# A graph layer on one core: rows of x by ScalarE's queue for five groups more, the sigmoid of the distances further back, and two gather buffers fewer

## The chip, the cores and the metric

The kernel runs on one core of a Trainium2 chip. The metric is the device time of one execution in microseconds (us), lower is better; the time of a kernel is the median of several executions. The core has five engines that run side by side: TensorE (PE; its weight loads are listed as PEld), VectorE (DVE), ScalarE (ACT), GpSimd (POOL) and SyncE (SP). An engine works through its own instructions in order. Transfers (DMAs) are issued by SP, ACT or POOL and announce their landing by semaphores.

## The reference

One message-passing layer over a graph with N = 12500 nodes and 200000 edges that are sorted by their target, followed by a residual and a layer norm. ssp(x) is softplus(x) - ln 2.

```python
gates = ssp(edge_attr @ We1 + be1) @ We2 + be2
gates = gates * (1 - sigmoid(5 * (distance - 3.5)))
h = ssp(concat(x[src], x[dst]) @ Wn1 + bn1) @ Wn2 + bn2
sums = zeros_like(x).at[dst].add(h * gates)
new = x + ssp(sums @ Ws1 + bs1) @ Ws2 + bs2
out = layernorm(x + new)
```

All is float32. `distance` is called `dist` in the kernel, and 1 - sigmoid of it is kept in the tile `cut`.

## The kernel before

**Groups.** Edges go in NG = 391 groups of 512, each as K = 4 columns of 128 edges. For group g the kernel needs the 512 rows x[src]: they go to a tile `xg` of 128 x 4 x 128 numbers, 64 of each 128 being a row of x, and 42 a one-hot code of the edge's target inside a window (`onehot`, L219). POOL fetches them by indirect DMA, one for each column (`gather`, L186), from the indices `src_i`. `gather` runs AHEAD = 16 groups in front of the group at work, and `xg` has AHEAD + BEHIND = 20 buffers. In one group of every 32 (the slots: 36, 68, ..., 388, twelve of them) only three columns are gathered. The 128 rows of the fourth are read by SP as plain DMAs of one row, ROWS = 4 in each step (`fetch`, L197 and L201), in the 32 steps before, to a tile `xr`; the row numbers come from the tile `rows_i` by a register load. In such a group `onehot` copies the code to `xr` (L221).

**A step** of the main loop works on several groups at once, in an order written out by hand. TensorE's order in step i is: second layer on the edges of group i-1 (L269, L272), first layer of group i+1 (L236, L238 on the edge data `eT`, L244 on the transposed rows with the weights `wns`), `scatter` of group i-3 (L295, messages times one-hot code), transposes of group i+3 (L227), second layer on the nodes of group i-1 (L278). ScalarE takes the exponential (L255) and logarithm (L258) of the first layer's result `z` and copies the transposed rows (L232). VectorE makes softplus of them (L263), multiplies by `cut` (L287) and by the gate (L291), adds the scatter's windows to `sums` (L311). SP loads `eT` (L207) and two pieces of `wns` (L214) for group i+5. `wns` holds, below the weights of the source, 42 rows of a table that the kernel itself writes to memory before the loop: the target's part of the first layer, for each node.

A buffer of `xg` is free once its group's scatter has ended. In step i POOL is to gather group i+16 to the buffer of group i-4, whose scatter stands in step i-1.

**Node blocks.** When all edges of a block of 512 nodes are done, the last part of the reference (`node_block`, L330 to L390) is strewn over the steps that follow.

**The start.** Before the loop DVE finds each group's window, ScalarE prepares biases, and TensorE computes the table in 14 pieces (PARTS = 7 parts of two, L508). ScalarE (L510) and DVE (L511) copy each piece from PSUM, SP stores it (L512), and DVE clears a stretch of `sums` (L513), where the input of that piece had lain. Gathers start here too: the first FREE = 7 groups at once, and the other nine of the AHEAD groups each behind a piece of the table, by a memset on DVE (L181) that the gather waits for:

```python
waiting.setdefault(min(5 * (g - FREE) // 3, 2 * PARTS - 1), []).append(g)
```

Ahead of the first piece stands the sigmoid of the distances (L498 to L501): DVE, ScalarE with a load of the sigmoid's table, a load of the table for exponential and logarithm, DVE. After the sixth piece (part 2) DVE computes the targets relative to their windows, `rel` (L524, L527).

Of the kernel before, what the change touches and what calls it, by code (L numbers as in the profile page):

```python
# [42 lines left out]
F32 = mybir.dt.float32  # L43
BF16 = mybir.dt.bfloat16
I32 = mybir.dt.int32
AF = mybir.ActivationFunctionType
OP = mybir.AluOpType
# [2 lines left out]
DRAM = bass.MemoryType.DRAM  # L50
DVE = mybir.EngineType.DVE
SP = mybir.EngineType.SP


Part = namedtuple("Part", "tensor others")

P = 128
D = 64
# [4 lines left out]
PIECES = 3  # L63
NB = 512
K = 4
AHEAD = 16
LOADS = 5
SPREADS = 5
CATCH_UP = 10
PREPARE = 5  # L70
FREE = 7
BEHIND = 4


BLOCK_STEPS = ((2, 3, 4, 4, 6, 7, 8, 9, 10, 14), (2, 3, 3, 4, 5, 6, 7, 8, 9, 10), (1, 2, 1, 2, 3))
ROWS = 4
CUTOFF = 5.0
EPS = 1e-5
LN2 = 0.6931471805599453
# [20 lines left out]

def slots_by_rows(NG):

    return [g for g in range(P // ROWS + 4, NG - 2, P // ROWS)]


@with_exitstack
def gnn_resnorm_kernel(ctx: ExitStack, tc: tile.TileContext, a: dict, out: bass.AP, E: int):
    nc = tc.nc
    x = a["x"]
    N = x.shape[0]  # L110
    NG = a["eT"].shape[1]
# [10 lines left out]
    loads = ctx.enter_context(tc.tile_pool(name="loads", bufs=LOADS + 2))  # L122
# [26 lines left out]
    packed, at = {}, 0  # L149
# [17 lines left out]

    xgs, xrs, eTs = {}, {}, {}

    by_rows = slots_by_rows(NG)  # L170
    rows_i = const.tile([len(by_rows), P], I32, name="rows_i")

    def padding(g, k):
# [13 lines left out]
                out=xg[:, k, :D], out_offset=None, in_=x,  # L187
                in_offset=bass.IndirectOffsetOnAxis(ap=src_i[:, g, k : k + 1], axis=0))

    def fetch(i):  # L190

        n, r = divmod(i * ROWS, P)
        if i < 0 or n >= len(by_rows):
            return
        if r == 0:
            xrs[by_rows[n]] = loads.tile([P, P], F32, name="xr", bufs=2)
        _, at = nc.values_load_multi_w_load_instructions(  # L197
            rows_i[n : n + 1, r : r + ROWS], engines=[SP], min_val=0, max_val=N - 1,
            skip_runtime_bounds_check_because="src holds rows of x")
        for j, v in enumerate(at):  # L200
            nc.sync.dma_start(xrs[by_rows[n]][r + j : r + j + 1, :D], x[bass.ds(v, 1), :])  # L201

    bases = {}

    def load(g):
# [195 lines left out]
    with tc.manual_schedule():  # L401
# [4 lines left out]
        with tc.tile_pool(name="prep", bufs=1) as prep:  # L406
# [14 lines left out]
            dist = cut.rearrange("p g k -> p (g k)")  # L421
# [52 lines left out]
            for i, w in enumerate((we2[:D, 0, :], wn2)):  # L474
                n = w.shape[0]
# [16 lines left out]
            rows = prep.tile([PIECES, 4, D], BF16, name="rows")  # L492
# [2 lines left out]
                load_x(i)  # L495


            nc.vector.tensor_scalar(dist, dist, CUTOFF - 1.5, 5.0, OP.subtract, OP.mult)  # L498
            nc.scalar.activation(dist, dist, AF.Sigmoid)
            nc.scalar.preload_act_table_set("natural_log_exp_and_others")  # L500
            nc.vector.tensor_scalar(dist, dist, -1.0, 1.0, OP.mult, OP.add)  # L501
            by_node = table.rearrange("(p c) f -> p c f", c=NCH)
            for i in range(PARTS):
                for c in range(i * CP, (i + 1) * CP, CP // 2):
                    m = CP // 2
                    ps = z_tile().rearrange("p b (k f) -> p (b k) f", k=K)
                    for k in range(m):
                        nc.tensor.matmul(ps[:, k, :], xT[:, c + k, :], wnb, start=True, stop=True)  # L508
                    tb = prep.tile([P, m, 2 * D], F32, name="tb", bufs=6)
                    nc.scalar.copy(tb[:, :K, :], ps[:, :K, :])  # L510
                    nc.vector.tensor_copy(tb[:, K:, :], ps[:, K:m, :])  # L511
                    nc.sync.dma_start(by_node[:, c : c + m], tb)  # L512
                    nc.vector.memset(sums[:, c * P : WIDE if c + m == NCH else (c + m) * P], 0.0)  # L513
                    for g in waiting.get(c // m, []):
                        gather(g, after=True)
                if i == 1:
                    nc.vector.tensor_copy(base_i, base_b[:1])
                    for k in range(2):
                        nc.vector.tensor_copy(be3[:, k, :], rows[:, 0, :])
                    for k in range(K):  # L520
                        nc.vector.tensor_copy(row3[:, :, k, :], rows[:, 1:3, :])
                        nc.vector.tensor_copy(rs3[:, k, :], rows[:, 3, :])
                if i == 2:
                    nc.vector.tensor_copy(rel, dst_i)  # L524
                    for t in range(2):
                        r = rel[:, :, 2 * t : 2 * t + 2]
                        nc.vector.tensor_sub(r, r, base_b[:, :NH].rearrange("p (g h) -> p g h", h=2))  # L527


        with tc.tile_pool(name="finish", bufs=1) as finish:  # L530
# [24 lines left out]
            for i in range(-3, last - 1):  # L555
                now = parts.pop(i, [])
                early = [part for part in now if part.tensor]
                at(load, i + LOADS)
                fetch(i)
                if i >= 0:  # L560
                    at(gather, i + AHEAD, i < BEHIND)
                if i < ends:
                    for g in second[i]:
                        layer2_edge(g)
                    if i >= -1:
                        zs[i + 1] = z_tile()
                        layer1_edge(i + 1)
                        for part in early:
                            part.tensor(tx_tile())
                    if i >= -1:  # L570
                        layer1_node(i + 1)
                    for n, g in enumerate(third[i]):
                        scatter(g, zs[i + 1][:, 1, HE + 2 * W * n : HE + 2 * W * (n + 1)])
                    at(exps, i + 1)
                    at(logs, i + 1)
                    for g in ahead[i]:
                        transposes(g)
                        xcopy(g)
                    for g in second[i]:
                        layer2_node(g)  # L580
                    for g in second[i]:
                        hcut(g)
                        message(g)
                    for g in third[i]:
                        window(g)
                    for part in early:
                        part.others()
                    at(softplus, i + 1)
                else:
                    for g in ahead[i]:  # L590
                        transposes(g)
                        xcopy(g)
                    zs[i + 1] = z_tile()
                    layer1_edge(i + 1)
                    for part in early:
                        part.tensor(zs[i + 1][:, 1, HE:])
                    layer1_node(i + 1)
                    exps(i + 1)
                    logs(i + 1)
                    for g in second[i]:  # L600
                        layer2(g)
                        hcut(g)
                        message(g)
                    softplus(i + 1)
                    for g in third[i]:
                        scatter(g, tx_tile()[:, : 2 * W])
                        window(g)
                    for part in early:
                        part.others()
                for g in ahead[i]:  # L610
                    at(onehot, g + 2)
                for part in now:
                    if not part.tensor:
                        part.others()
                complete = third[i][-1] + 1 if third[i] else 0
                if blocks and complete >= blocks[0][1] - PREPARE and not begun:
                    begun = node_block(*blocks[0][0], finish)
                    begun.pop(0).others()
                if blocks and complete >= blocks[0][1]:
                    steps = next(steps for steps in BLOCK_STEPS if i + steps[-1] < last - 1)  # L620
                    for n, part in zip(steps, begun):
                        parts.setdefault(i + n, []).append(part)
                    rest = begun[len(steps) :]
                    blocks.pop(0)
                    begun = None
# [38 lines left out]
            for part in begun:  # L664
# [4 lines left out]
                         skip_runtime_bounds_check_because="a comparison's result")  # L669
    with tc.If(far > 0), tc.tile_pool(name="outside", bufs=1) as o:  # L670
# [7 lines left out]
        with tc.For_i(0, NG, 1) as g:  # L678
# [14 lines left out]
            for k in range(K):  # L693
                for i in range(2):
                    nc.gpsimd.indirect_dma_start(
                        out=xg[:, k, i, :], out_offset=None, in_=x,
# [20 lines left out]
            v = gh.rearrange("p (i k d) -> p i k d", i=2, k=K)  # L717
# [27 lines left out]
def layouts(inputs):  # L745
# [3 lines left out]
    x = np.asarray(inputs["x"])  # L749
    src, dst = (np.asarray(inputs[n]) for n in ("src", "dst"))  # L750
    dist = np.asarray(inputs["edge_weight1"])[:, 0]
    edge = np.asarray(inputs["edge_attr_64"])
    N, E = x.shape[0], src.shape[0]
    NG = -(-E // GE)
# [9 lines left out]

    out = {"x": np.ascontiguousarray(x)}
    out["src_l"] = lanes(src, 0)
    out["rows"] = np.ascontiguousarray(out["src_l"].reshape(P, NG, K)[:, slots_by_rows(NG), K - 1].T)
    out["dst_l"] = lanes(dst, dst[-1])
    out["dist_l"] = lanes(dist, 1e6)
    out["dst_h"] = np.ascontiguousarray(padded(dst, NR * P * HE, dst[-1]).reshape(NR, P, HE).transpose(1, 0, 2))  # L770
# [4 lines left out]
    steps = block_steps(N, NG)  # L775
# [37 lines left out]
```

## Time and profile before

| what | value |
|---|---|
| time before, median of 3 runs | 2487.79 us (2479.47 to 2490.7) |
| the profiled execution | 2482.05 us, of which the span of the profile is 2480.3 us |
| mean granted TensorE clock | 0.861 |
| gathers on POOL (L186) | 1551, 950 ns each |
| rows by SP's plain DMAs (L201) | 1536 |
| first copy of a table piece, last copy | at 33.92 us, at 87.35 us |
| first and last exponential of the main loop's groups (L255) | at 99.34 us, at 2460 us |

A page gives each engine's busy time with its share of the span, the costliest groups of instructions (source line, engine, operation, tiles, count, then busy time, mean ns of one, idle time of the engine before them and what ended it), and the chain of work that ended last. A timeline's line starts with the start in us and the duration in us, and ends with the idle time before, in brackets, with what ended it; "remote" there is a release that the profile couldn't name. A table by stretches gives, for each stretch, its length, the busy time and number of instructions of PE, PEld, DVE, ACT and POOL, then the granted clock, the DMA share and GB/s. Starts of TensorE's matmuls are recorded, their ends modelled.

### The profile page before, as it was taken

The page shows a single profiled execution, that of the slowest core. Times are in us where ns is not written, and L with a number is a line of the kernel's source. Part 1 is how long each engine was busy: PE and PEld are TensorE (multiplying, and loading weights), DVE is VectorE, ACT ScalarE, POOL GpSimd, SP SyncE. Part 2 cuts the span into 40 slices and gives each one's busy share as a digit, 9 for nine tenths or more (in the row PEclk, how much of TensorE's full clock was granted, in tenths as well). Part 3 has the DMA queues.
Part 4 walks back from the last instruction along what each step waited for, and adds up shares of the span by engine and source line. Part 5 has one row for each costly group of instructions (what it writes and reads, how often), then busy time and mean ns, then how long its engine had stood idle before and what let it go on. Part 6 is the DMA issues. An engine that isn't in the chain of part 4 may idle for free.

```text
span 2480.3 us, 41084 instructions
## 1 busy us (share of the span) xinstructions
PE 2138.7 (86%) x11373; PEld 1741.1 (70%) x11373; DVE 1087.5 (44%) x2744; ACT 920.1 (37%) x1317; POOL 1473.3 (59%) x1555
## 2 busy tenths in 40 slices
PE   3888898889888989888988988888889888888897
PEld 3767677777767777767767776677767676676775
DVE  3334434444344344444444444444444444444455
ACT  1223333333333333433433333433333333433443
POOL 6656666666666666666666666666665656666620
PEclk9988879887888878898897888988887989988898
DMA  6322222222222222222222222222222222222220
GB/s 187 111 50 53 51 51 52 53 52 51 53 51 55 53 51 53 55 53 53 55 54 56 52 53 55 55 56 55 53 57 55 50 55 56 57 60 55 55 53 22
DMA packets 170982, 143.07 MB, mean 58 GB/s; under 512 B 46475, under 2 KB 142915, under 8 KB 170746
## 3 DMA queue, kind: packets, MB, share of 16 engines
q1 hardware_dynamic: 119746, 87.95, 12.3%
q0 software_dynamic: 49632, 50.92, 11.5%
q10 hardware_dynamic: 1368, 1.51, 0.3%
q8 instruction: 93, 1.52, 0.3%
q14 instruction: 143, 1.17, 0.2%
HBM read 130.57 MB, written 9.63 MB: 57 GB/s over the span
## 4 chain that ended last, share of the span: by engine, by line
PE 79%; issue 9%; DVE 5%; ACT 3%; another core or an unknown queue 3%; DVEq 1%; DMA 1%; SPq 0%; ACTq 0%
PE z L244 17%; PE gh L278 12%; PE gh L272 11%; PE z L238 11%; PE tx L227 8%; PE z L295 8%; PE gh L269 4%; PE z L236 3%; PE tx L330 2%; DVE h L287 1%; DVE msg L291 1%; ACT u L255 1%; DVE sums L311 1%; PE z L508 1%
## 5 line engine op out<-in xcount | busy, mean ns | idle before, releaser
L186 POOL DMA_INDIRECT xg<-in_x,src_i x1551 | 1473.1, 950 | 909.8 <-issue 360.3
L255 ACT ACTIVATE u<-z 128x768 f32<-128x768 f32 x392 | 317.4, 810 | 1435.4 <-PE z L244 466.8
L287 DVE TENSOR_TENSOR h<-gh,cut 128x256 f32<-128x256 f32 x391 | 166.0, 425 | 1154.0 <-PE z L244 357.8
L244 PE MATMUL z<-xT,wns 106*128 106x256 f32 x1564 | 498.4, 448 | 3.8 <-issue 1.6
L278 PE MATMUL gh<-consts,s 128*128 128x64 f32 x3128 | 429.6, 285 | 7.4 <-issue 7.4
L278 PEld LDWEIGHTS gh<-consts,s 128*128 128x128 f32 x3128 | 424.1, 210 | 6.9 <-issue 6.8
L272 PE MATMUL gh<-consts,s 128*128 128x128 f32 x1564 | 308.9, 325 | 133.8 <-issue 124.4
L244 PEld LDWEIGHTS z<-xT,wns 106*128 106x128 f32 x1564 | 353.0, 227 | 72.7 <-issue 4.2
L272 PEld LDWEIGHTS gh<-consts,s 128*128 128x128 f32 x1564 | 227.6, 210 | 240.4 <-issue 224.8
L263 DVE SCALAR_TENSOR_TENSOR s<-u,z 128x768 f32<-128x768 f32 x392 | 372.7, 951 | 24.3 <-ACT u L258 12.3
L258 ACT ACTIVATE u<-u,one 128x768 f32<-128x768 f32 x392 | 365.9, 934 | 12.7
L227 PE MATMUL tx<-consts,xg 128*106 128x128 f32 x1552 | 279.9, 308 | 61.0 <-ACT u L258 25.6
L238 PE MATMUL z<-eT,consts 128*128 128x256 f32 x782 | 313.9, 487 | 0.0
L295 PEld LDWEIGHTS z<-xg,msg 128*128 128x128 f32 x1512 | 279.8, 230 | 41.1 <-issue 8.2
L295 PE MATMUL z<-xg,msg 128*128 128x84 f32 x1512 | 263.4, 301 | 14.5 <-issue 14.2
L227 PEld LDWEIGHTS tx<-consts,xg 128*106 128x106 f32 x1552 | 211.3, 160 | 86.8 <-issue 46.0
L232 ACT COPY xT<-tx 106x512 f32<-106x512 f32 x391 | 221.6, 567 | 18.4 <-PE tx L227 11.2
L311 DVE TENSOR_TENSOR sums<-sums,z 64x42 f32 x756 | 148.7, 197 | 129.9 <-issue 118.4
L291 DVE TENSOR_TENSOR msg<-gh,h 128x256 f32<-128x256 f32 x391 | 165.8, 424 | 13.4
L238 PEld LDWEIGHTS z<-eT,consts 128*128 128x128 f32 x782 | 131.4, 211 | 54.1 <-issue 15.4
L269 PE MATMUL gh<-row,ones 3*128 3x512 bf16 x391 | 157.1, 402 | 2.7 <-DVE msg L291 2.6
L219 DVE TENSOR_TENSOR xg<-consts,rel 128x168 f32<-128x168 f32 x391 | 137.0, 351 | 0.1
(100 smaller groups left out, 621.4 us busy)
## 6 DMA issues: line engine op xcount, KB each, us to landing
eT<-in_eT SPq DMA_DIRECT2D x391, 128.0 KB
xg<-in_x,src_i POOLq DMA_INDIRECT x1551
xr<-in_x SPq DMA_DIRECT2D x1536, 0.2 KB
wns<-table SPq DMA_DIRECT2D x782, 21.0 KB
table<-tb SPq DMA_DIRECT2D x14, 448.0 KB
sums<-in_xT SPq DMA_DIRECT2D x7, 455.0 KB
y<-in_x SPq DMA_DIRECT2D x24, 128.0 KB
out<-y SPq DMA_DIRECT2D x24, 128.0 KB
```

What stands on the lines that cost most here:

```text
L186: nc.gpsimd.indirect_dma_start(out=xg[:, k, :D], out_offset=None, in_=x, in_offset=bass.IndirectOffsetOnAxis(ap=src_i[:, g, k : k + 1], ax ...
L227: nc.tensor.transpose(tx[:, k, :], row, ident)
L232: nc.scalar.copy(xT, xTs[g])
L238: nc.tensor.matmul(zs[g][:, 0, :HE], we1.rearrange("a h d -> a (h d)"), eTs[g], start=False, stop=True, skip_group_check=True)
L244: nc.tensor.matmul(zn, wns[:, g % REST, h, :], xTs[g][:, h], start=True, stop=True, skip_group_check=True)
L255: nc.scalar.activation(us[g][:, part], z_of(g)[:, part], AF.Exp)
L258: nc.scalar.activation(us[g][:, part], us[g][:, part], AF.Ln, bias=one)
L263: nc.vector.scalar_tensor_tensor(ss[g].rearrange("p i t e -> p (i t e)")[:, part], us[g][:, part], BIG, z_of(g)[:, part], OP.min, OP.max)
L269: nc.tensor.matmul(gh, ones3[:, :P], row3.rearrange("q i k d -> q (i k d)"), start=True, stop=False, skip_group_check=True)
L272: nc.tensor.matmul(v[:, 0, t], ss[g][:, 0, t, :], we2, start=False, stop=False, skip_group_check=True)
L278: nc.tensor.matmul(ghs[g][:, 1, 2 * t + h, :], ss[g][:, 1 + h, t, :], wn2, start=False, stop=h == 1 and t == 1, skip_group_check=True)
L295: nc.tensor.matmul(sc, msgs[g][:, 2 * t : 2 * t + 2, :].rearrange("p h f -> p (h f)"), xgs[g][:, 2 * t : 2 * t + 2, D:DW], start=t == 0, s ...
```

## The change

- Beside the slots that SP fills, ScalarE's queue fills others: one in every 64 groups, from group 69 (69, 133, 197, 261, 325), with ACT_ROWS = 2 rows of x in each step. `fetch` takes the queue as an argument; for ScalarE the row numbers of four steps (8) are loaded to registers at once. In these groups POOL gathers three columns too. Each of the two kinds has an `xr` tile of its own, with two buffers.
- AHEAD goes from 16 to 14, so `xg` has 18 buffers, and the first of the two loads of indices is for 14 groups. FREE goes from 7 to 5; nine groups still wait for table pieces.
- The sigmoid of the distances stands behind the table's sixth piece, ahead of `rel`.

```diff
-AHEAD = 16
+AHEAD = 14
-FREE = 7
+FREE = 5
+ACT_ROWS = 2
...
-    return [g for g in range(P // ROWS + 4, NG - 2, P // ROWS)]
+    return [list(range(P // n + 4 + (n == ACT_ROWS), NG - 2, P // n)) for n in (ROWS, ACT_ROWS)]
...
-    by_rows = slots_by_rows(NG)
+    sp_rows, act_rows = slots_by_rows(NG)
+    by_rows = sp_rows + act_rows
...
-    def fetch(i):
+    def fetch(i, slots, some, engine, queue, first, steps=1):
 
-        n, r = divmod(i * ROWS, P)
-        if i < 0 or n >= len(by_rows):
+        n, r = divmod(i * some, P)
+        if i < 0 or n >= len(slots):
             return
+        g = slots[n]
         if r == 0:
-            xrs[by_rows[n]] = loads.tile([P, P], F32, name="xr", bufs=2)
-        _, at = nc.values_load_multi_w_load_instructions(
-            rows_i[n : n + 1, r : r + ROWS], engines=[SP], min_val=0, max_val=N - 1,
-            skip_runtime_bounds_check_because="src holds rows of x")
-        for j, v in enumerate(at):
-            nc.sync.dma_start(xrs[by_rows[n]][r + j : r + j + 1, :D], x[bass.ds(v, 1), :])
+            xrs[g] = loads.tile([P, P], F32, name=f"xr{first}", bufs=2)
+        if i % steps == 0:
+            _, numbers[first] = nc.values_load_multi_w_load_instructions(
+                rows_i[first + n : first + n + 1, r : r + some * steps], engines=[engine], min_val=0, max_val=N - 1,
+                skip_runtime_bounds_check_because="src holds rows of x")
+        for j, v in enumerate(numbers[first][i % steps * some :][:some]):
+            queue.dma_start(xrs[g][r + j : r + j + 1, :D], x[bass.ds(v, 1), :])
...
-            nc.vector.tensor_scalar(dist, dist, CUTOFF - 1.5, 5.0, OP.subtract, OP.mult)
-            nc.scalar.activation(dist, dist, AF.Sigmoid)
-            nc.scalar.preload_act_table_set("natural_log_exp_and_others")
-            nc.vector.tensor_scalar(dist, dist, -1.0, 1.0, OP.mult, OP.add)
...
                 if i == 2:
+                    nc.vector.tensor_scalar(dist, dist, CUTOFF - 1.5, 5.0, OP.subtract, OP.mult)
+                    nc.scalar.activation(dist, dist, AF.Sigmoid)
+                    nc.scalar.preload_act_table_set("natural_log_exp_and_others")
+                    nc.vector.tensor_scalar(dist, dist, -1.0, 1.0, OP.mult, OP.add)
                     nc.vector.tensor_copy(rel, dst_i)
...
-                fetch(i)
+                fetch(i, sp_rows, ROWS, SP, nc.sync, 0)
+                fetch(i, act_rows, ACT_ROWS, ACT, nc.scalar, len(sp_rows), 4)
```

More of the change, by code (lines that the diff above doesn't have):

```diff
@@ L52 @@
 SP = mybir.EngineType.SP
+ACT = mybir.EngineType.Activation
 Part = namedtuple("Part", "tensor others")
@@ L168, in gnn_resnorm_kernel @@
     xgs, xrs, eTs = {}, {}, {}
-    by_rows = slots_by_rows(NG)
+    sp_rows, act_rows = slots_by_rows(NG)
+    by_rows = sp_rows + act_rows
+    assert len(set(by_rows)) == len(by_rows)
     rows_i = const.tile([len(by_rows), P], I32, name="rows_i")
@@ L188, in gather @@
                 in_offset=bass.IndirectOffsetOnAxis(ap=src_i[:, g, k : k + 1], axis=0))
-    def fetch(i):
-        n, r = divmod(i * ROWS, P)
-        if i < 0 or n >= len(by_rows):
+    def fetch(i, slots, some, engine, queue, first, steps=1):
+        n, r = divmod(i * some, P)
+        if i < 0 or n >= len(slots):
             return
+        g = slots[n]
         if r == 0:
-            xrs[by_rows[n]] = loads.tile([P, P], F32, name="xr", bufs=2)
-        _, at = nc.values_load_multi_w_load_instructions(
-            rows_i[n : n + 1, r : r + ROWS], engines=[SP], min_val=0, max_val=N - 1,
-            skip_runtime_bounds_check_because="src holds rows of x")
-        for j, v in enumerate(at):
-            nc.sync.dma_start(xrs[by_rows[n]][r + j : r + j + 1, :D], x[bass.ds(v, 1), :])
+            xrs[g] = loads.tile([P, P], F32, name=f"xr{first}", bufs=2)
[5 more added lines that the diff above has]
+            queue.dma_start(xrs[g][r + j : r + j + 1, :D], x[bass.ds(v, 1), :])
+    numbers = {}
     bases = {}
@@ L766, in layouts @@
     out["src_l"] = lanes(src, 0)
-    out["rows"] = np.ascontiguousarray(out["src_l"].reshape(P, NG, K)[:, slots_by_rows(NG), K - 1].T)
+    out["rows"] = np.ascontiguousarray(out["src_l"].reshape(P, NG, K)[:, sum(slots_by_rows(NG), []), K - 1].T)
     out["dst_l"] = lanes(dst, dst[-1])
```

## The prediction

> **What bounds the kernel now.** I read the page first, then the timeline of ScalarE (ACT) and GpSimd (POOL) over a few groups, then the busy times by stretch, then the start. The page suggests TensorE:
>
> ```profile
> PE 2138.7 (86%) x11373; PEld 1741.1 (70%) x11373; DVE 1087.5 (44%) x2744; ACT 920.1 (37%) x1317; POOL 1473.3 (59%) x1555
> PE 79%; issue 9%; DVE 5%; ACT 3%; another core or an unknown queue 3%; DVEq 1%; DMA 1%; SPq 0%; ACTq 0%
> L186 POOL DMA_INDIRECT xg<-in_x,src_i x1551 | 1473.1, 950 | 909.8 <-issue 360.3
> L255 ACT ACTIVATE u<-z 128x768 f32<-128x768 f32 x392 | 317.4, 810 | 1435.4 <-PE z L244 466.8
> ```
>
> The first exponential of each group (L255) marks the pace. POOL around step 180, where the group being gathered (196) is a slot that takes three gathers instead of four:
>
> ```profile
> 1191.49 0.94 POOL L186 DMA_INDIRECT xg<-in_x,src_i  x1 [1.40 <-PE z L236]
> 1192.74 0.95 POOL L186 DMA_INDIRECT xg<-in_x,src_i  x1 [0.30 <-issue]
> 1193.99 0.95 POOL L186 DMA_INDIRECT xg<-in_x,src_i  x1 [0.30 <-issue]
> 1195.24 0.94 POOL L186 DMA_INDIRECT xg<-in_x,src_i  x1 [0.31 <-issue]
> 1197.51 0.94 POOL L186 DMA_INDIRECT xg<-in_x,src_i  x1 [1.32 <-PE z L244]
> 1198.76 0.95 POOL L186 DMA_INDIRECT xg<-in_x,src_i  x1 [0.30 <-issue]
> 1200.01 0.94 POOL L186 DMA_INDIRECT xg<-in_x,src_i  x1 [0.30 <-issue]
> 1202.18 0.94 POOL L186 DMA_INDIRECT xg<-in_x,src_i  x1 [1.22 <-PE z L244]
> ```
>
> The busy times of the same three steps (cut at the starts of L255), and of three steps at the end when no gather is left:
>
> ```profile
> 1191.26:1197.27 6.01, 6.01 (x38) 5.04 (x37) 2.47 (x6) 2.53 (x4) 3.78 (x4) 1.00 0.23 51
> 1197.27:1201.94 4.67, 3.86 (x27) 3.18 (x26) 2.81 (x7) 2.22 (x3) 2.84 (x3) 1.00 0.19 35
> 1201.94:1208.03 6.09, 5.51 (x36) 4.55 (x36) 2.44 (x6) 2.62 (x6) 3.78 (x4) 1.00 0.22 51
> 2391.91:2396.26 4.35, 4.35 (x30) 3.66 (x29) 2.69 (x7) 2.22 (x3) 0.00 (x0) 1.00 0.20 58
> 2396.26:2401.06 4.80, 4.80 (x34) 4.11 (x33) 2.52 (x7) 2.54 (x5) 0.00 (x0) 1.00 0.16 44
> ```
>
> So a step's length follows the number of gathers: four 6.05 us (the median over the loop), three 4.67, none 4.35 to 4.80, with the clock at 1.00 in all of them. The slot steps 20, 52, 84, 116, 148, 180, 212, 244, 276 and 340 lie between 4.58 and 4.78. POOL issues every 1.25 us, then waits about 1.3 us for the scatter that frees its buffer; TensorE, ScalarE and POOL go on at the same moment. The work around it is elastic: steps with a node block's extra exponentials, or with its y load or its store on SP, have medians of 6.07, 6.05 and 6.02 us; only the step with L330 is longer (6.55).
>
> Where rule and trace part: the Trainium skill (Perfetto Trace Analysis, Identifying the Most-Contended Engine) calls the engine of highest occupancy the most contended, and counts weight loads for TensorE: 70% against POOL's 59%. By it a gather less is worth nothing. By the rows it is worth 6.05 - 4.68 = 1.37 us. I follow the rows; the rule's sum is a rival below.
>
> The start is the second place:
>
> ```profile
> 33.92 0.59 ACT L510 COPY tb<-z 128x512 f32<-128x512 f32 x1
> 41.30 0.59 ACT L510 COPY tb<-z 128x512 f32<-128x512 f32 x1 [6.80 <-remote]
> 53.99 1.07 ACT L510 COPY tb<-z 128x512 f32<-128x512 f32 x2 [12.10 <-remote]
> 87.35 0.59 ACT L510 COPY tb<-z 128x512 f32<-128x512 f32 x1 [2.40 <-PE z L508]
> ```
>
> These copies of table pieces wait for TensorE alone. Pieces 2 and 3 had ended by 24.2 and 38.5, yet their copies begin at 41.30 and 53.99. POOL gathers without a pause from 3.29 to 49.99 (7 free groups, then two that pieces 1 and 2 release), 36 gathers. Once it has paused, copies follow at 3.0 us, TensorE's pace. So a long run of gathers holds back the ends of matmuls as ScalarE sees them.
>
> **The change part by part.** (1) *Five slots more* (groups 69, 133, 197, 261, 325; the words say six, the list gives five): gathers fall from 1551 to 1546. 5 x 1.37 = **-6.9 us**. The five extra 0.19 us copies of L221 are beside other work.
>
> (2) *AHEAD 16 to 14*, with BEHIND at 4, so 18 buffers. POOL still waits for the scatter of four groups back, so the steady step stays. But the last gather is issued in step 376 instead of 374: two steps of 6.05 take the place of 4.80 and 4.35: **+3.0 us**.
>
> (3) *FREE 7 to 5*: eight gathers fewer before the table ends. The first run is 20 gathers, 3.3 to 28.3. POOL then idles until piece 1 is copied.
>
> (4) *Sigmoid behind the sixth piece*. ScalarE's stream has its rows DMA at 29.52, a table load that the build puts in (1.28 us, as before), then the first copy at 31.1 instead of 33.92. DVE writes the memset that frees the next gathers at about 33.1. Piece 2, its signal freed by POOL's pause, is copied at 32; piece 3 ends at 35.7, piece 4 at 38.8, each copied at once if eight gathers (33.4 to 43.4) are too few to hold signals back: before, some 13 gathers after the pause at 50 passed without harm (copies at 61.59 to 73.54 every 3.0 us), and the next copy came 3.2 us late (79.74). Then 3.0 us a piece: the sixth at 44.8. Now sigmoid: on ScalarE 1.28 + 1.51 + 1.28 us, with DVE's 0.98 on each side and its rel operations (0.97 + 1.86) behind; DVE copies piece 7 at 53.1 instead of 50, which makes TensorE 3.3 us late. Eight pieces follow, 24 us, with these 3.3 and some 4 us (0 to 9) of held signals: the last copy at about 76.3 (72 to 81) instead of 87.35: **-11 us**. The first reader of the result, L287, comes after 100 us.
>
> (5) *ScalarE's rows*: 640 one-row DMAs in 320 steps, two between the copy of xT and the next exponential, and a register load of eight numbers in every fourth. Row: SP's four take 2.6 to 3.4 us while POOL gathers, 1.5 without gathers, and the load before them 0.55. So ScalarE has 1.3 to 1.7 us a step and 0.6 more in every fourth. It idles 1435.4 / 392 = 3.66 us before the exponential: covered. If its two rows took over 3.6 us, each us beyond would cost 320. In a slot step the gap is 2.4 us: some 17 x 1/4 x 0.5 = 2 us at most. I take **+0.5**. Queued behind the rows are exponential, logarithm and copy; DVE's softplus, then TensorE's L272 and L244 wait for these.
>
> The rows share the eight landing semaphores with SP's loads: an ACT row mostly waits for an SP row of one step back, and 422 of SP's DMAs wait for an ACT row, most of one step back. SP loads five groups ahead (load k+5 leaves within 1.6 us of exponential k), so there are 30 us of cover. At the start there is less: SP's load k+5 left 6 to 13 us after exponential k for k = 0 to 6. There ScalarE may wait for SP's late rows: from 0 to +6; I take **+1.5**, for SP catches up by step 7.
>
> Rule and row again: the skill (DMA: Bandwidth & Descriptors, Issuing engines are not separate DMA queues) says that issuing from several engines saves only the sequencer's issue time. By it ScalarE's queue brings no faster transfer, and the two rows are 2 x 0.4 us of issue without contention. The row while POOL gathers says twice that. Neither reaches the gap, so the sum is the same.
>
> Sum: -6.9 + 3.0 - 11 + 0.5 + 1.5 = -12.9. The profiled execution took 2482.05 (span 2480.3 and 1.75 around it), so 2469.2. The median shown, 2487.79, stands 5.7 above the profiled one; on that scale **2475 us**. A measurement of this kernel tells about 0.5% from no change, 12.4 us: the forecast sits on that edge.
>
> **The rivals.** *ScalarE's rows lengthen the step (slower).* Four gathers at 1.37 leave 0.57 us of the 6.05; were that SP's seven DMAs, 0.08 each, two more would add 0.16 us in 320 steps: +52, so 2475 + 52 = 2527. It decides from 12.9 / 320 = 0.04 us a step. Against: y loads and stores add a DMA to a step and leave it at 6.05 and 6.02. For: ScalarE issued no DMA in the loop before, and the exponential is behind these.
>
> *Occupancy is right*: slots and later end count nothing, only the start: -11 + 2 = -9: 2479. Against: the slot steps.
>
> *The start gives nothing*: signals are held anyway, and sigmoid stalls the table: 0 + 3.3 - 6.9 + 3.0 + 2 = +1.4: 2489. For: 56 of the 64 gathers in front remain. Against: signals passed at once after the pause at 50.
>
> *ScalarE and SP lock*: SP's rows wait for ACT's and these for SP's; if the round of two steps passes 12.1 us, every step grows. From the rows about 7 us of SP, 1 + 2 of ScalarE and landing: 10, so it holds. If not, +0.3 us a step, near +100: 2570.
>
> **How the numbers follow.** Main case 0.58 (own range 2462 to 2484: faster by over 0.5% 0.33, within 0.25); occupancy 0.08 (0.02, 0.06); start 0.11 (within 0.08, slower 0.03); rows lengthen 0.18 (within 0.02, slower 0.16); lock 0.05 (slower). Together faster 0.35, same 0.41, slower 0.24. The range 2460 to 2510 leaves out the far part of the slower cases and little below.
>
> **What would show it.** Right: slot steps 55, 119, 183, 247, 311 near 4.7 us, the others at 6.05; the last table copy near 76; the last gather two steps before the fast tail; ScalarE's gap filled by some 1.5 us of issue. Wrong: steps above 6.1 from group 1 to 320, a gap of ScalarE gone, SP's lead shrinking below five groups, or the last table copy still after 84.

## The result, and the profile after

The changed kernel takes **2669.8 us** (median of 4, 2658.99 to 2674.81), the kernel before 2483.63 beside it (4 runs): a ratio of **1.0738** (95% interval 1.0705 to 1.077), 186 us slower. The forecast was 2475. The profiled execution's span is 2666.6 us, 186.3 above that of before.

The page after, the lines that answer to those of before and the two of the first layer on `eT` (line numbers have moved: gather L186 to L190, exponential L255 to L262, transposes L227 to L234, `eT`'s matmul L238 to L245, rows L201 to L207, `eT` L207 to L214, `wns` L214 to L221):

```profile
PE 2259.3 (85%) x11373; PEld 1808.2 (68%) x11373; DVE 1085.5 (41%) x2749; ACT 923.1 (35%) x1318; POOL 1469.3 (55%) x1550
L190 POOL DMA_INDIRECT xg<-in_x,src_i x1546 | 1469.1, 950 | 1101.1 <-PE tx L234 399.7
L262 ACT ACTIVATE u<-z 128x768 f32<-128x768 f32 x392 | 317.3, 810 | 1537.6 <-PE z L302 462.1
L245 PE MATMUL z<-eT,consts 128*128 128x256 f32 x782 | 326.3, 505 | 99.5 <-DMA eT<-in_eT 95.3
L245 PEld LDWEIGHTS z<-eT,consts 128*128 128x128 f32 x782 | 136.1, 218 | 161.0 <-DMA eT<-in_eT 111.2
```

There are five gathers less, as counted. POOL's idle time grew from 909.8 to 1101.1 us and ScalarE's from 1435.4 to 1537.6. New is that TensorE waits for SP's transfers. The largest four such groups in the waits after (total us, times, longest); before, none of them was above 1.4 us:

```profile
PEld z L245 <- DMA eT<-in_eT: 111.2, 80, 5.4
PE z L245 <- DMA eT<-in_eT: 95.3, 71, 5.3
PE tx L234 <- DMA wns<-table: 53.6, 5, 11.3
PE tx L234 <- DMA xr<-in_x: 44.6, 6, 10.5
```

(The first two are much the same time, seen by weight loads and by matmuls. The transposes at L234 don't read `wns`: those five waits are the slot steps 34, 66, 162, 194 and 226, put down to another transfer.) The distances between exponentials say where the 186 us lie; step k is the time from the first exponential of group k to that of group k+1. The start is 9.1 us shorter (first exponential at 90.20 in place of 99.34); from exponential 0 to 34 the loop loses 8.0; from 34 to 320 it loses 161.9; from there to the last exponential 22.3; the rest is 3.3 longer. Of the 161.9, 105.1 lie in nine single steps, 34, 66, 98, ... 290: they take 14.4 to 20.0 us, where before eight of them took 6.04 to 6.16 (step 226 took 2.15, and the next one 11.1). These are the steps in which TensorE transposes SP's slots (36, 68, ...). The tenth, 322, takes 15.2. After it, when ScalarE has no rows left, steps are about 6.05 again.

One of the nine, step 130, from the timeline (start us, us, engine, line; idle before). The four SP rows that start at 952.28 are the last of slot 132:

```profile
944.20 0.49 PE L234 MATMUL tx<-consts,xg 128*106 128x128 f32 x3
946.08 0.81 ACT L262 ACTIVATE u<-z 128x768 f32<-128x768 f32 x1 [3.83 <-PE tx L234]
947.80 1.51 SPq L207 DMA_DIRECT2D xr<-in_x  x4
952.28 1.50 SPq L207 DMA_DIRECT2D xr<-in_x  x4
954.89 0.16 PEld L234 LDWEIGHTS tx<-consts,xr 128*106 128x106 f32 x1 [10.46 <-DMA xr<-in_x]
954.92 0.43 PE L234 MATMUL tx<-consts,xr 128*106 128x128 f32 x1 [10.24 <-DMA xr<-in_x]
```

TensorE has done the three gathered columns by 944.7 and stands for 10.2 us until the fourth lands. The table by stretches, cut at the exponentials of steps 129 to 131 (length, then PE, PEld, DVE, ACT, POOL, clock, DMA share, GB/s), shows the whole core idle for much of the long one:

```profile
940.00:946.08 6.08, 4.11 (x22) 3.04 (x22) 2.66 (x7) 2.22 (x3) 3.79 (x4) 1.00 0.16 32
946.08:962.04 15.96, 7.12 (x27) 5.67 (x28) 3.23 (x8) 2.33 (x3) 3.78 (x4) 0.57 0.19 51
962.04:968.07 6.03, 6.03 (x42) 5.04 (x41) 2.44 (x6) 3.04 (x6) 3.79 (x4) 1.00 0.23 52
```

The other 56.8 us lie mostly in steps of 7 to 11 us (37 of them, before 11), but not in the waits for `eT` themselves: the 69 steps in which TensorE waits over 0.3 us for a DMA take 6.13 us on average. Often it is the next step that is long. Step 217, with a wait, and the two after it:

```profile
1524.71 1.22 PE L245 MATMUL z<-eT,consts 128*128 128x256 f32 x2 [2.06 <-DMA eT<-in_eT]
1522.70:1528.76 6.06, 4.05 (x12) 3.18 (x13) 2.47 (x6) 2.22 (x4) 3.78 (x4) 0.64 0.24 51
1528.76:1536.72 7.96, 7.96 (x30) 6.42 (x29) 2.44 (x6) 2.22 (x4) 3.78 (x4) 0.50 0.18 44
1536.72:1542.86 6.14, 6.14 (x40) 5.45 (x38) 2.44 (x6) 2.22 (x4) 3.79 (x4) 0.89 0.33 75
```

In step 218 TensorE is busy throughout, at a granted clock of 0.50. Worked out from the trace between exponentials 34 and 320 (a slot step isn't counted as a next step): behind the 45 steps with a DMA wait of 1 us or more, the next step has a mean clock of 0.71 and takes 6.76 us; behind the 201 steps with no wait over 0.3 us, 0.88 and 6.19; behind the nine slot steps, 0.75 and 7.01. Counted beyond 6.05 us, some 48 of the 56.8 are in steps with a clock of 0.60 or less (59 with a mean of 6.98 us; before, 41 with 6.22). That the waits lower the clock fits these figures; no run here separates the two.

The start itself came nearly as forecast, on ScalarE:

```profile
50.62 0.59 ACT L513 COPY tb<-z 128x512 f32<-128x512 f32 x1 [6.62 <-remote]
53.66 1.51 ACT L528 ACTIVATE cut<-cut 128x1564 f32<-128x1564 f32 x1 [1.16 <-DVE cut L527]
56.48 1.07 ACT L513 COPY tb<-z 128x512 f32<-128x512 f32 x2
78.30 0.59 ACT L513 COPY tb<-z 128x512 f32<-128x512 f32 x1 [2.40 <-DVE sums L516]
```

The last table copy begins at 78.30 in place of 87.35.

**Why SP is late.** Right after the slot step, SP and then ScalarE on the timeline of after:

```profile
972.56 2.35 SPq L207 DMA_DIRECT2D xr<-in_x  x4
977.21 1.49 SPq L221 DMA_DIRECT2D wns<-table  x2
979.43 4.11 SPq L207 DMA_DIRECT2D xr<-in_x  x4
983.63 0.36 SPq L214 DMA_DIRECT2D eT<-in_eT  x1
...
975.11 0.61 ACTq L207 DMA_DIRECT2D xr<-in_x  x2
981.29 0.62 ACTq L207 DMA_DIRECT2D xr<-in_x  x2
```

ScalarE's two rows cost ScalarE 0.61 us. But SP's four take 4.11 us from 979.43: the third waits for the semaphore on which ScalarE issued a row at 981.29, and leaves at 982.89, 1.6 us after it. Every DMA of both queues takes the next of eight landing semaphores, in the order in which the built program lists them, and waits until the transfer before it on that semaphore has landed. The trace has the semaphore of each issue: from the loop's first step on, 3391 issues of both queues can be merged into one sequence that goes through the eight in turn, and in one way only.

The waits view puts little of this down to ScalarE's rows; the gaps between SP's instructions show it. The Trainium skill (Perfetto Trace Analysis, DMA Instruction — HWDGE (DVE, Sync)) says that an issue's reported start comes after its semaphore wait, so that a wait lies ahead of the issue and not in it; the trace agrees, SP's instructions took 3.83 us a step before and 3.82 after. Worked out from the trace, for each SP instruction that waits on one of the eight: the idle time just before it, sorted by the queue that used the semaphore last.

| kernel, stretch | after SP's own transfer: number, mean us, over 0.8 us | after ScalarE's row: number, mean us, over 0.8 us | the latter, us a step |
|---|---|---|---|
| before, 300 to 2000 us | 1986, 0.09, none | - | - |
| after, 300 to 2000 us | 1473, 0.10, none | 346, 0.52, 67 of 141.5 us in all | 0.70 |

Both columns together are 0.67 us a step before and 1.29 after, +0.62; the mean step of this stretch grew from 6.09 to 6.64 us, +0.55. (As SP's instructions take the same time, its gaps must grow as the step does; what the table adds is where they grew.) In steps 34 to 321, 70 of the 73 long waits lie in the first 13 steps after a slot step. So SP, which has caught up while TensorE stood still (at exponential 35 it has issued the rows of 34 steps), is held back some 2 us a step for ten steps, until it is four steps behind (at exponential 44 the rows of 40 steps, at 56 of 52). Before, it stood within a step (43.75 at 44, 55.75 at 56, 199 at 200). The distance is much the same in the sequence that the semaphores give, three to five steps: ScalarE's rows of 60 steps end there behind SP's of 55, and those of 200 behind 197.

### The profile page after: what moved, and what is told of

Read it like the earlier page. It is cut to its first block, busy times and chain, and to the rows that moved or that the text cites. A ratio compares the mean times of both kernels' runs of the same rounds, so it can differ in the third digit from the quotient of the medians.

```text
span 2666.6 us, 43082 instructions
## 1 busy us (share of the span) xinstructions
PE 2259.3 (85%) x11373; PEld 1808.2 (68%) x11373; DVE 1085.5 (41%) x2749; ACT 923.1 (35%) x1318; POOL 1469.3 (55%) x1550
## 3 DMA queue, kind: packets, MB, share of 16 engines
q14 instruction: 158, 1.29, 0.2%
## 5 line engine op out<-in xcount | busy, mean ns | idle before, releaser
L190 POOL DMA_INDIRECT xg<-in_x,src_i x1546 | 1469.1, 950 | 1101.1 <-PE tx L234 399.7
L262 ACT ACTIVATE u<-z 128x768 f32<-128x768 f32 x392 | 317.3, 810 | 1537.6 <-PE z L302 462.1
L251 PE MATMUL z<-xT,wns 106*128 106x256 f32 x1564 | 539.5, 473 | 34.7 <-issue 16.9
L285 PE MATMUL gh<-consts,s 128*128 128x64 f32 x3128 | 462.6, 298 | 21.7 <-issue 21.7
L285 PEld LDWEIGHTS gh<-consts,s 128*128 128x128 f32 x3128 | 457.6, 224 | 22.3 <-issue 22.3
L245 PE MATMUL z<-eT,consts 128*128 128x256 f32 x782 | 326.3, 505 | 99.5 <-DMA eT<-in_eT 95.3
L279 PE MATMUL gh<-consts,s 128*128 128x128 f32 x1564 | 318.6, 333 | 46.6 <-issue 34.2
L279 PEld LDWEIGHTS gh<-consts,s 128*128 128x128 f32 x1564 | 235.5, 216 | 153.8 <-issue 126.7
L302 PEld LDWEIGHTS z<-xg,msg 128*128 128x128 f32 x1512 | 294.6, 242 | 39.4 <-issue 3.0
L234 PE MATMUL tx<-consts,xg 128*106 128x128 f32 x1547 | 288.4, 318 | 17.3 <-issue 5.2
L302 PE MATMUL z<-xg,msg 128*128 128x84 f32 x1512 | 272.7, 313 | 1.8 <-issue 1.5
L245 PEld LDWEIGHTS z<-eT,consts 128*128 128x128 f32 x782 | 136.1, 218 | 161.0 <-DMA eT<-in_eT 111.2
L234 PEld LDWEIGHTS tx<-consts,xg 128*106 128x106 f32 x1547 | 225.8, 169 | 23.9 <-issue 9.2
L276 PE MATMUL gh<-row,ones 3*128 3x512 bf16 x391 | 165.8, 424 | 9.5 <-DVE msg L298 4.4
L298 DVE TENSOR_TENSOR msg<-gh,h 128x256 f32<-128x256 f32 x391 | 166.0, 425 | 13.5
```

The costliest lines, as they stand in the source:

```text
L190: nc.gpsimd.indirect_dma_start(out=xg[:, k, :D], out_offset=None, in_=x, in_offset=bass.IndirectOffsetOnAxis(ap=src_i[:, g, k : k + 1], ax ...
L234: nc.tensor.transpose(tx[:, k, :], row, ident)
L245: nc.tensor.matmul(zs[g][:, 0, :HE], we1.rearrange("a h d -> a (h d)"), eTs[g], start=False, stop=True, skip_group_check=True)
L251: nc.tensor.matmul(zn, wns[:, g % REST, h, :], xTs[g][:, h], start=True, stop=True, skip_group_check=True)
L262: nc.scalar.activation(us[g][:, part], z_of(g)[:, part], AF.Exp)
L279: nc.tensor.matmul(v[:, 0, t], ss[g][:, 0, t, :], we2, start=False, stop=False, skip_group_check=True)
```

## The experiments

The theory, called the **chain**: the eight semaphores are dealt in the listed order, SP stands four steps behind ScalarE in it, and so a landing holds SP there; SP's slots, whose last rows have two steps of cover, stop TensorE, and `eT`, with five groups, comes just late. Rivals: **contention** (two more transfers a step slow SP's issue or its transfers), **buffers** (AHEAD, FREE, the moved sigmoid), **SP's own rate** (SP's round is the loop's, whatever the order).

Chips differ. The first four kernels (e1 to e4) ran on one where the kernel before takes 1998.2 us, not 2484; three of them ran again (e5 to e7) where it takes 2484.9. For e8 to e11 it takes 2463.83, for e12 2458.36. Ratios are against the kernel before, run beside it.

### ScalarE's rows taken away, and the old start put back

```diff
-    return [list(range(P // n + 4 + (n == ACT_ROWS), NG - 2, P // n)) for n in (ROWS, ACT_ROWS)]
+    return [list(range(P // ROWS + 4, NG - 2, P // ROWS)), []]
```

is e1 and e6. e2 is after with FREE = 7 and the four lines of the sigmoid ahead of the first piece again.

> The kernel after, without ScalarE's rows: POOL gathers the five slots again; AHEAD 14, FREE 5 and the moved sigmoid stay. Chain theory (a row on ScalarE's queue shares the eight landing semaphores with SP's transfers, in an order fixed when the program is built, and in that order SP stands four steps behind ScalarE, so SP can no longer run ahead) and contention theory (two more transfers a step slow SP's issue) both expect the forecast's start and end: about 2480 us (2470 to 2490), no step of 14 us or more, no TensorE wait for eT. Buffer theory (AHEAD 14 and FREE 5 or the moved sigmoid starve the loop) expects 2600 or more with the long steps still there.

> ScalarE's rows with the sigmoid back in its old place and FREE 7; AHEAD stays 14, for which there is room. Chain and contention theories expect the loss of after in full, plus the start that is not gained: 2680 us (2665 to 2695), ten steps of 14 to 20 us. Buffer theory expects about 2490 if FREE and the sigmoid were to blame.

> As e1 (no rows on ScalarE's queue, the rest of the change in place). Where before takes about 2484: chain and contention theories 2480 us (2470 to 2490); buffer theory 2600 or more. Where before takes 1998: as before within 1%.

e6: 2486.33 us, ratio 1.0003 (0.9989 to 1.0017); the slot steps up to 322 take 6.0 to 6.2 us, and TensorE's `eT` waits come to 0.2 us. So the loss needs ScalarE's rows, and **buffers** falls.

On the first chip e1 has a ratio of 1.0029 (1.0014 to 1.0044) and e2 of 0.9999 (0.9983 to 1.0015): the totals tell nothing there, since POOL alone sets them:

```profile
L190 POOL DMA_INDIRECT xg<-in_x,src_i x1546 | 1466.0, 948 | 478.9 <-issue 322.0
```

In e2, 478.9 us of idle time before 1546 gathers is 0.31 each, the pause that stands even inside a run of gathers: POOL never stops. But its trace is the cleanest of all. The largest of SP's waits for TensorE in e1, and then of those for rows in e2:

```profile
SPq L214 <- PE z L245: 142.5, 199, 3.0
SPq L221 <- PE tx L234: 100.2, 289, 1.2
```

```profile
SPq L221 <- DMA xr<-in_x: 72.3, 43, 3.2
SPq L207 <- DMA xr<-in_x: 47.2, 36, 4.3
SPq L214 <- DMA xr<-in_x: 27.1, 21, 5.8
```

SP's instructions take 3.37 us a step in e1 and 3.35 in e2 (220 to 1600 us), so nothing slows the issue: **contention** of the issue falls. Nor do the transfers slow down: by the landings in the traces, a row of SP lands 1.01 us after its issue in e1 and 1.04 in e2, an `eT` 1.79 in both (medians). In the loop e1's SP waits for TensorE to free buffers. In e2 it waits for `xr` rows as well: after SP's own transfers 1627 gaps with a mean of 0.04 us, after ScalarE's rows 381 with 0.40, 71 of them over 0.8. At exponential 56 e2's SP has the rows of 52 steps, e1's of 54, and e2's slot steps take 15.6 to 18.4 us, where e1's take 4.35 to 5.23.

### Six rows a step, swapped: four by ScalarE, two by SP; and four by ScalarE alone

```diff
-ROWS = 4
-ACT_ROWS = 2
+ROWS = 2
+ACT_ROWS = 4
```

(e3 and e5; the row numbers are loaded for two steps at once.) In e11, ScalarE's four rows are alone: `[[], list(range(P // ACT_ROWS + 5, NG - 2, P // ACT_ROWS))]`.

> Six rows a step and sixteen slots as in after, but ScalarE fetches four of the rows and SP two. In the built program SP now stands four groups ahead of ScalarE, not four behind, because SP has two transfers less a step. Chain theory expects the loss to vanish: 2473 us (2460 to 2490), eT issued well ahead of its exponential, no step above 9 us. Contention theory expects the loss of after or more, since ScalarE issues twice as many rows: 2660 or above. If the loss is SP's own count of transfers (nine in place of seven a step between the two queues), 2600 or above as well.

> The swap of e3 (ScalarE four rows a step, SP two) once more, since the chip of e1 to e4 ran the kernel before in 1998 us and so showed nothing of steps of 6.05 us. Where before takes about 2484: chain theory 2473 us (2460 to 2490), no step above 9 us, as SP stands four groups ahead of ScalarE in the built program; contention theory 2660 or above. Where before takes 1998: no change within 1%.

> Four rows a step by ScalarE alone, none by SP: eleven slots, as before had. SP has three transfers a step and stands four groups ahead of ScalarE in the built program, as in e5. Chain theory: no step of 14 us; what is left is what ScalarE waits for landings itself: 2500 us (2480 to 2530) where before takes 2484. Contention theory, by twice the rows of after on ScalarE's queue: 2650 or above.

e3, on the first chip, has a ratio of 0.9999 (0.9983 to 1.0014). e5 took 2526.23 us, 1.0168 (1.0151 to 1.0185): as many rows as after and twice as many on ScalarE, and 41 us of loss in place of 186. From step 34 on no step is over 12.4 us, and TensorE's `eT` waits come to 0.4 us. So the number of ScalarE's rows isn't what costs: contention falls again. That SP has two transfers less would explain e5 as well as its place in the list does; the gaps and e2, where SP has time to spare, tell these two apart. And 2473 was a miss. The chain holds both ways, and now ScalarE is the one held: between 300 and 2000 us, 281 of its 646 rows that follow a transfer of SP on their semaphore leave after a gap over 0.8 us, 1 of the 455 that follow a row of its own. Its exponential's line in e5:

```profile
L262 ACT ACTIVATE u<-z 128x768 f32<-128x768 f32 x392 | 317.0, 809 | 1471.6 <-DMA xr<-in_x 490.7
```

e11 missed its 2480 to 2530 as well: 2549.94 us, ratio 1.0353 (1.0287 to 1.0418). From step 34 on it has no step of 14 us, but 30 steps above 9 us between 35 and 320, 122 us beyond 6 us each. One of them, ScalarE and then SP:

```profile
630.27 0.81 ACT L262 ACTIVATE u<-z 128x768 f32<-128x768 f32 x1 [2.49 <-DMA xr<-in_x]
632.61 7.34 ACTq L207 DMA_DIRECT2D xr<-in_x  x4
...
628.06 1.48 SPq L221 DMA_DIRECT2D wns<-table  x2
636.81 0.36 SPq L214 DMA_DIRECT2D eT<-in_eT  x1
```

SP's `eT`, which waits for TensorE to free its buffer, leaves at 636.81; ScalarE's second row, next on the same semaphore, leaves at 638.96, and the next exponential stands behind it. Why this falls so often in e11 and seldom in e5 I did not test.

### More cover for SP's slots

```diff
+    return [list(range(P // n + (9 if n == ROWS else 5), NG - 2, P // n)) for n in (ROWS, ACT_ROWS)]
```

> SP's slots five steps later (41, 73, ... in place of 36, 68, ...), so that their last row has seven steps of cover in place of two; all else as after. Chain theory expects SP still four steps behind, so the ten long steps lose their excess (some 11 us each) and the steps of 7 to 8 us at eT stay: 2560 us (2540 to 2580). A theory that SP's own round of about 6.5 us is the rate of the loop expects what the slots give back to come again as waits for eT: 2640 or above.

> As e4 (SP's slots five steps later). Where before takes about 2484: chain theory 2560 us (2540 to 2580), the ten long steps gone and the waits for eT left; the theory that SP's round is the rate 2640 or above. Where before takes 1998: as before within 1%.

e4, on the first chip: 1.001 (0.9995 to 1.0024). e7: 2603.97 us, 1.048 (1.0456 to 1.0504), between the two expectations: a third of the loss goes. No slot step is long any more, but TensorE waits for `eT` more often than in after, 112 times in place of 71:

```profile
PEld z L245 <- DMA eT<-in_eT: 177.9, 123, 3.2
PE z L245 <- DMA eT<-in_eT: 153.4, 112, 3.0
```

SP is still four steps behind (64 at exponential 68). Here too the long steps are those behind the waits: between exponentials 34 and 320, the steps after the 85 with a DMA wait of 1 us or more have a mean clock of 0.72 and take 6.94 us, those after the 179 with none over 0.3 us 0.87 and 6.19. So cover takes the slot steps out, and waits for the next transfer with the least of it stay. How they divide between chain and SP's rate, this run leaves open.

### SP held back without any row of ScalarE, and six rows on SP

```diff
-        eTs[g] = loads.tile([P, HE], F32, name="eT")
+        eTs[g] = loads.tile([P, HE], F32, name="eT", bufs=2)
```

on top of e6 is e9. e10 is after with `ACT_ROWS, SP, nc.sync` in the second `fetch`.

> As e6 (no rows on ScalarE's queue), with two buffers for eT in place of seven, so that SP's transfer of group k waits for TensorE to be done with group k-2: SP is held some three steps behind ScalarE with no transfer added. Chain theory expects a good part of the loss of after, at the same places: the steps 34, 66, 98 ... longer by 4 to 10 us each, 2545 us (2520 to 2600) where before takes 2484. Contention theory (a late SP isn't the cause, ScalarE's transfers are) expects 2486 as e6, with no long steps.

> The same sixteen slots as after, all six rows a step on SP and none on ScalarE: nine transfers a step on one queue. SP's step is 5.6 to 6.0 us for seven transfers while gathers run, so nine would take about 7.5 us and set the loop: some 1.4 us a step, 2484 + 450 = 2930 us (2800 to 3050) where before takes 2484. If SP's stalls under gathers are the larger part and don't grow with its transfers: 2600.

e9: 2558.89 us, ratio 1.0389 (1.0347 to 1.0431), 95 us lost with no transfer added. SP is three steps behind (65.0 at exponential 68), and the slot steps take 9.6 to 14.9 us:

```profile
PE tx L234 <- DMA xr<-in_x: 46.6, 7, 8.5
```

So SP's lateness is enough for the long steps, whatever makes it late. e10, a single run: 2745.59 us where before takes 2463.83, better than the 2930 forecast and 282 us worse than before; its slot steps take 14 to 21 us and TensorE waits for `eT`:

```profile
PEld z L245 <- DMA eT<-in_eT: 159.9, 93, 4.4
PE z L245 <- DMA eT<-in_eT: 138.6, 85, 4.2
PE tx L234 <- DMA xr<-in_x: 112.0, 10, 14.5
```

The picture of after, made by SP's own work: **SP's own rate** is a real limit, and SP has no room for two rows more. ScalarE's queue did spare SP the issue, and then gave much of it back as waits.

### One row a step in place of two

```diff
-ACT_ROWS = 2
+ACT_ROWS = 1
```

> As after, with one row a step on ScalarE's queue in place of two (slots 133 and 261 alone, so rows until step 255): half the dose. Chain theory: SP stands four steps behind ScalarE in the built program as in after, and one row a step holds it there as well as two, so the slot steps up to 258 stay at 14 to 20 us (eight of them, some 90 us) and some eT waits come: ratio to before about 1.05 (1.04 to 1.065), that is 2590 us where before takes 2464 to 2484. Contention theory (cost by the row): two fifths of the rows of after, so two fifths of its loss: ratio 1.03 or below, with slot steps no longer than 10 us.

2590.95 us, ratio 1.0522 (1.0415 to 1.0628): as the chain expected. Up to exponential 256 half of after's rows cost 72% of its loss (against the profile of before, from 0 to 256 after lost 132 us and this kernel 95). From exponential 34 to 256 SP's gaps after ScalarE's rows are 0.74 us a step, where after has 0.69: 187 gaps with a mean of 0.88 us in place of 298. The slot steps up to 258 take 13.5 to 18.5 us. One row a step holds SP as well as two.

### The start alone

The kernel before with FREE = 5 and the sigmoid behind the sixth piece, AHEAD 16:

> The kernel before with the sigmoid behind the sixth piece and FREE 5 alone: AHEAD 16 and 20 buffers stay, no rows on ScalarE's queue. e6 began 8.6 us earlier than before and ended level, with its last gather 8.6 us later; so if AHEAD 14 took that back, this kernel keeps the start: 2476 us (2470 to 2481) where before takes about 2484. If the start is worth nothing because the loop gives it back whatever AHEAD is: 2484 (within 0.2%).

2467.57 us, ratio 1.0003 (0.9979 to 1.0027): the second expectation. Its first exponential is at 87.8 us (99.34 in the profile of before, whose runs took 2484), but the total doesn't move. No run points to a version that beats the kernel before.

## Why the prediction was wrong

- **The failed step is in (5)**: "422 of SP's DMAs wait for an ACT row, most of one step back. SP loads five groups ahead ... so there are 30 us of cover." It failed twice. "One step back" was counted in the built program's list, and there SP stands four steps behind ScalarE; on the chip it had stood within a step, so that the row it waits for had yet to be issued. And the five groups of lead are what such a wait uses up; a thing that is taken can't be the cover. SP's own rows, moreover, never had five: their last are due two steps on.
- **The size.** No time was put on it. The ten slot steps alone cost 114 us, and SP's gaps grew by 0.62 us a step. SP had little to spare: before, between 300 and 2000 us, no gap ahead of an instruction that waits for a semaphore was over 0.8 us, and two rows a step more on it (e10) cost 282 us.
- **"ScalarE and SP lock"** was the right mechanism with 0.05 of the chance. It asked whether a round fits into two steps (10 of 12.1 us) and not what order the list prescribes. Its price, 0.3 us a step, was about half of what came: 186 us in 320 steps are 0.58.
- **ScalarE's own cost** was right in its end: ScalarE still idled before the exponential (1537.6 us in all, 1435.4 before). The two rows take 0.61 us, not 1.3 to 1.7: SP's durations under gathers didn't carry over. "Rows lengthen the step" by issue time did not happen.
- **The start** was right where it was forecast (78.30 for 76.3, inside 72 to 81; -9.1 for -11) and wrong as a term of the sum: e6 and e8 keep the earlier first exponential and their medians are level with the kernel before. Three parts of e6's profile, beside that of before, show where the lead of 8.7 us goes (e6's ends 6.7 us behind). POOL never had it: it idled until piece 1, its 29th gather begins at 42.6 us (before 40.3) and its last at 2391.0 (2382.4). By exponential 320 the lead is down to 2.2 us, for which no run gives the cause. Behind the last full exponential, that of group 389, e6 has a granted clock of 0.50 where before had 1.00 and then 0.65 (e6's two stretches first):

```profile
2454.26:2462.45 8.19, 8.19 (x29) 6.19 (x28) 3.19 (x8) 2.32 (x3) 0.00 (x0) 0.50 0.00 0
2462.45:2487.00 24.55, 13.02 (x47) 10.20 (x46) 8.53 (x28) 4.74 (x12) 0.00 (x0) 0.50 0.05 14
2454.62:2459.12 4.50, 4.50 (x29) 3.36 (x28) 2.64 (x7) 2.33 (x3) 0.00 (x0) 1.00 0.00 0
2459.12:2480.30 21.18, 9.50 (x47) 6.92 (x46) 8.98 (x30) 4.75 (x12) 0.00 (x0) 0.65 0.06 16
```

That is 7.1 us more, and it isn't AHEAD's: e8, with AHEAD 16, has the slow end too (33.2 us), and e5, e9 and e12, with 14, take 26.0 to 27.3 us there, near before's 25.7.
- **AHEAD** was forecast at +3.0. In e6 the last gather does stand in step 376 in place of 374, and from exponential 371 to 389 e6 takes 1.9 us longer than before.
- **Five slots**: the list's five gathers went (1546), but steps 55, 119, 183, 247 and 311 took 5.5, 5.0, 8.1, 5.7 and 7.7 us (183 at a clock of 0.50, 311 at 0.78). Their 6.9 us were never measured by themselves, nor was the rival on occupancy. The prediction's list of slot steps also leaves out 308, which took 7.48.
- **The rule on issuing engines** (the Trainium skill, DMA: Bandwidth & Descriptors, Issuing engines are not separate DMA queues) was weighed only for speed, and rightly as far as it goes. It says that a second engine saves issue time; here the second queue also cost the first one 0.70 us a step in waits, of which that section says nothing. The measurement decides.
- Of the signs named, two came: steps above 6.1 us until step 320, and SP's lead gone. The third, ScalarE's gap gone, came only in the swap.

## What to carry to other kernels

Before a second queue is given transfers, ask which landing semaphores it will share with the first and in what order they are dealt; if the first runs ahead of that order, it will be held to it, and one transfer a step is enough. Look for the engine that fills its step with small gaps, though it is never listed as busy: it has nothing to give to a wait. Take the cover of a transfer from the last one that is due, not from the one with the most lead. When TensorE waits, look at the granted clock of the step behind the wait too: part of the loss may stand there.

## What the runs showed of the hardware

- The same kernel takes 1998 us on one chip and 2458 to 2485 on the others. On the first SP's register moves take 29 ns with hardly a spread (e1: 90% at or below 29); on the others, under the same gathers, about a tenth of them take over 0.65 us (e6, the moves for rows). On the first, POOL's gathers never stop and set the time: 1551 times 1.25 us are 1939. On the others, POOL waits about 1.3 us in each step.
- On the first chip ten long steps cost nothing in the total (e2): POOL, 14 groups ahead, goes on gathering, with 0.31 us before each gather. A stall is only lost on the way that sets the end.
- In after, a step at a granted clock of 0.50 takes 8.1 us with TensorE busy throughout (59, 163, 227, 259), and 6.05 at 1.00. Such steps stand mostly behind a wait: 18 of the 26 steps over 7 us with a clock of 0.60 or less come right after a slot step or a step with a DMA wait of 1 us or more (e7: 31 of 42).
